# The scores of a whole batch: two pairs of heads per turn instead of one, in a cross-attention and FFN layer

## The chip, the core and the metric

The kernel runs on one core of one Trainium2 chip. The metric is the device time of one execution in microseconds (us). The engines are TensorE (PE in the profile, its weight loads PEld), VectorE (DVE), ScalarE (ACT), GpSimd (POOL) and SyncE (SP), which issues most of the DMAs.

## What is computed

A transformer layer on 32 batches of 100 rows of 256 values: cross attention of 16 heads of 64 over 361 context rows, then a feed-forward part of 1024 with int8-style quantization, each behind a layer norm and with a residual. Only the attention matters here:

```python
def _L0_xattn_ref(Q, K, V, WQ, WK, WV, WO, mask):
    B, T, D, H, DK, DV = (4, 512, 256, 16, 64, 64)
    Qh = jnp.einsum('btd,hdk->bhtk', Q, WQ)
    Kh = jnp.einsum('btd,hdk->bhtk', K, WK)
    Vh = jnp.einsum('btd,hdv->bhtv', V, WV)
    dk = jnp.asarray(Qh.shape[-1], Qh.dtype)
    logits = jnp.einsum('bhtk,bhsk->bhts', Qh, Kh) / jnp.sqrt(dk)
    logits = logits + mask * -1000000000.0
    attn = jax.nn.softmax(logits, axis=-1)
    Ah = jnp.einsum('bhts,bhsv->bhtv', attn, Vh)
    A = jnp.transpose(Ah, (0, 2, 1, 3)).reshape(Ah.shape[0], Ah.shape[2], -1)
    return A @ WO
...
x = x + _L0_xattn_ref(_layernorm(x, axis=-1), ctx_1024, ctx_1024, L0_xattn_WQ, ...
x = x + _L0_ffn_ref(_layernorm(x, axis=-1), L0_ffn_W1, L0_ffn_b1, L0_ffn_W2, L0_ffn_b2)
return x
```

x is (32, 100, 256), the context (32, 361, 256), the mask (1, 1, 100, 361); all of the attention is in float32.

## The kernel before

The heads are taken as eight pairs (NHP = 8), one head of a pair on SBUF partitions 0 to 63, the other on 64 to 127. The work on the batches is cut into 36 steps: batches 1 to 30 are one step each with all eight pairs ("whole-batch steps", n == NHP), batch 0 is three steps of 2, 2 and 4 pairs, batch 31 three of 4, 2 and 2. The loop over the steps (L616) issues for each step, in this order: scores(i), attend(i - 1), the values v of this batch (v_part), queries and projections where they are due, and the keys of the next step (k_part). TensorE runs its instructions in exactly this written order (manual_schedule at L598); the other engines' queues are ordered by the compiler, with extra edges from follow(a, b), which puts a behind b on its engine.

One softmax is spread over two steps. In step i, scores(i) multiplies queries and keys (tile sc, L423), adds the mask and takes the row's extreme on VectorE (tiles p and m, L434), takes exponentials on ScalarE (L404) and scales them by the reciprocals of their sums on VectorE (L443, L449). Before attend can multiply with v, the probabilities have to be transposed: weights_T(i - 1, pair) does this one step later, on TensorE (tile pt, L373), 12 transposes of a pair into two tiles, and copies the two tiles to SBUF (pT, L385), both copies on ScalarE, but the first of pair 0 on VectorE. p is one buffer for all pairs: the masked scores of a pair go where the transposes of the same pair of the step before have just read.

A whole-batch step works in turns (turns is true): in each turn the transposes of one pair of the step before, then the scores of one pair of this one, eight times. The step after one of four pairs (step 3, batch 1) has transposes in its first four turns only. In the smaller steps all transposes come first, and then the scores, two pairs (PAIRS = 2) at a time. In whole-batch steps the exponentials of all 16 heads come after the last turn, and each follows the last ScalarE copy of the transposes (copied, L408).

All PSUM tiles of the attention come from one pool of eight banks (L162, function bank at L191), one bank for each tile whatever its size. A tile beyond the eighth waits until an earlier one has been read for the last time: pt by its copy (L385), sc by the mask instruction (L434), which ends with a read of its accumulator into m.

A score product of one head is two instructions in the profile (two passes of a float32 product), so one pair's scores are x4; the two heads of a pair run side by side on the two halves of the array's rows, and so do two of a pair's transposes.

Of the kernel before, what the change touches and what calls it, by code (L numbers as in the profile page):

```python
# [27 lines left out]
def kernel(  # L28
# [31 lines left out]
    PAIRS = 2  # L60
# [34 lines left out]
    def follow(a, b):  # L95

        tc.add_manual_dep(a.ins, b.ins.name, ORDER)
# [61 lines left out]
    with ExitStack() as att:  # L159
# [31 lines left out]
        def bank(name):  # L191
            return psum.tile([P, 512], F32, tag="ps", name=name)
# [50 lines left out]
        for b in range(B):  # L243
            first = 0
# [118 lines left out]
        def weights_T(i, pair, on_vector):  # L363

            h0 = 2 * pair
            pts = [bank(f"pt{i}_{pair}_{k}") for k in range(2)]
            for h in range(2):
                for c in range(NSC):  # L370
                    for k in range(2):
                        ks = slice(k * RH, k * RH + TH)
                        nc.tensor.transpose(  # L373
                            pts[k][:SC, (h * NSC + c) * TH : (h * NSC + c + 1) * TH],
                            pb[ks, h0 + h, c * SC : (c + 1) * SC],
                            ident[ks, ks],
                        )
            pT = pTs[i, pair] = p1.tile(
                [SC, 2 * NSC, 2, TH], F32, tag=f"pT{pair}", name=f"pT{i}_{pair}"
            )  # L380
            copies = []
            for k in range(2):
                src = pts[k][:SC, : 2 * NSC * TH].rearrange("p (c t) -> p c t", t=TH)
                copy = nc.vector.tensor_copy if k == 0 and on_vector else nc.scalar.copy
                copies.append(copy(pT[:, :, k, :], src))  # L385
            return copies

        def scores(i):

            b, first, n = steps[i]
            g, j = b // G, b % G
            _, p0, before = steps[i - 1] if i else (0, 0, 0)
            turns = n == NHP
            heads = range(2 * first, 2 * (first + n))
            rsum = small.tile([TP, 2 * NHP], F32, tag="rsum", name=f"rsum{i}")
            r = small.tile([TP, 2 * NHP], F32, tag="r", name=f"r{i}")
            ms = {}

            def exponentials(heads):
                for h in heads:
                    s = pb[:, h, :S]
                    done = nc.scalar.activation(  # L404
                        s, s, AF.Exp, bias=ms[h], scale=-1.0, accum_out=rsum[:, h : h + 1]
                    )
                    if turns:
                        follow(done, copied)  # L408

            if not turns:  # L410
                for pair in range(p0, p0 + before):
                    weights_T(i - 1, pair, True)
            for pairs in ([q] for q in range(first, first + n)) if turns else (
                range(q, q + PAIRS) for q in range(first, first + n, PAIRS)
            ):
                if turns and pairs[0] < before:
                    copied = weights_T(i - 1, p0 + pairs[0], pairs[0] == 0)[1]
                pss = {}
                four = range(2 * pairs[0], 2 * pairs[-1] + 2)
                for h in four:  # L420
                    pair, k = divmod(h, 2)
                    pss[h] = bank(f"sc{i}_{h}")
                    nc.tensor.matmul(  # L423
                        pss[h][:TP, :S],
                        qbuf[pair // PAIRS][
                            k * DK : (k + 1) * DK, pair % PAIRS, j, :, :
                        ].rearrange("p k t -> p (k t)")[:, :TP],
                        kT[k * DK : (k + 1) * DK, pair, :],
                        start=True,
                        stop=True,  # L430
                    )
                for h in four:
                    ms[h] = small.tile([TP, 1], F32, tag=f"m{h}", name=f"m{i}_{h}", bufs=1)
                    found = nc.vector.tensor_tensor_reduce(  # L434
                        pb[:, h, :S], pss[h][:TP, :S], maskt, 1.0, BIG, ALU.add, ALU.min, ms[h]
                    )
                if not turns:
                    exponentials(four)
            if turns:
                exponentials(heads)  # L440
            at_once = 1 if i == len(steps) - 1 else 4
            for h0 in heads[::at_once]:
                last = nc.vector.reciprocal(  # L443
                    r[:, h0 : h0 + at_once], rsum[:, h0 : h0 + at_once]
                )
                follow(last, found)
                for h in range(h0, h0 + at_once):
                    s = pb[:, h, :S]
                    nc.vector.tensor_scalar(s, s, r[:, h : h + 1], None, ALU.mult)  # L449
            return last  # L450

        def attend(i, pairs=None):


            b, first, n = steps[i]
            if pairs is not None:
                first, n = pairs
            g, j = b // G, b % G
            if first == 0 and j == 0:
                aTs[g] = p1.tile([P, NHP, G, T], F32, tag="aT", name=f"aT{g}")  # L460
            for p0 in range(first, first + n, HP):
                m = min(HP, n)
                av = bank(f"av{i}_{p0}")
                for pair in range(p0, p0 + m):
                    for c in range(NSC):
                        for k in range(2):
                            h = 2 * (pair % HP) + k
                            nc.tensor.matmul(  # L468
                                av[k * DK : (k + 1) * DK, (pair - p0) * T : (pair - p0 + 1) * T],
                                vs[b, pair // HP][:, c, h * DK : (h + 1) * DK],  # L470
                                pTs[i, pair][:, k * NSC + c, :, :].rearrange("p k t -> p (k t)"),
                                start=(c == 0),
                                stop=(c == NSC - 1),
                            )
                copied = nc.scalar.copy(
                    aTs[g][:, p0 : p0 + m, j, :],
                    av[:, : m * T].rearrange("p (c t) -> p c t", t=T),
                )
            return copied
# [136 lines left out]
        for i, (b, first, n) in enumerate(steps):  # L616
            g, j = b // G, b % G
            begun = [h for h in range(2) if first <= h * HP < first + n]
            ended = [h for h in range(2) if first < (h + 1) * HP <= first + n]
            last = scores(i)  # L620
            if i >= 1:
                attend(i - 1)
            if b >= 1:
                for h in begun:
                    for c in range(NSC):
# [3 lines left out]
                        if c != 2:  # L629
                            copied = done  # L630
# [33 lines left out]
        i = len(steps) - 1  # L664
# [5 lines left out]
        copied = attend(i, (NHP - 1, 1))  # L670
# [167 lines left out]
    for u, (g, n) in enumerate(units):  # L838
# [3 lines left out]
        for fc in range(NFC):  # L842
# [36 lines left out]
            if (u, fc) in rounded:  # L879
                i = rounded[u, fc]  # L880
# [125 lines left out]
```

## Time and profile before

| | us |
|---|---|
| median of 3 runs | 1338.23 (1337.56 to 1338.39) |
| the profiled execution | 1336.85 |
| its span, first to last instruction | 1335.1 |
| mean granted TensorE clock | 0.995 of full speed |

The costliest groups on TensorE, with the number of instructions, busy time and mean of one:

| line, work | instructions | busy us | mean ns |
|---|---|---|---|
| L287 v, 128x512 | 768 | 338.3 | 596 |
| L256 k, 128x361 | 1016 | 314.2 | 467 |
| L423 sc, 64x361 | 1024 | 208.5 | 490 |
| L468 av, 128x100 | 3072 | 140.0 | 250 |
| L373 pt, 50x50 | 3072 | 133.5 | 221 |

Matmuls overlap one another in the records, so that busy times and means are longer than what an instruction adds to the time; the distance from one start to the next is what counts. A whole-batch step's scores, from the first transpose to the first matmul of attend, take 8.31 us in 29 of the 30 steps (625.27 to 633.58 for batch 16) and 6.66 us in step 3 (from 56.49). VectorE's masks in them are 512 instructions in all (16 a batch) with a mean of 533 ns and an accumulator read of 82 ns each; ScalarE's copies of pt are 462 with a mean of 413 ns, VectorE's 50 with 468 ns.

The page gives busy time of each engine and its share of the span; the chain of waits follows the work that ended last back to the start, and can be cut to a stretch of time; the time line lists instructions in order of start, merged where equal ones follow each other (xN), with an engine's idle time before them and what ended it in brackets.

### The profile page before, as it was taken

Reading aid. Unit: us, or ns where it says so; the run is one execution under the profiler, and the core shown is the slowest. Engines: PE = TensorE matmul, PEld = TensorE weight load, DVE = VectorE, ACT = ScalarE, POOL = GpSimd, SP = SyncE. Lnnn points to the kernel's source line nnn. Section 1 sums busy time; section 2 is a strip of 40 time slices with the busy share of each in tenths; the row PEclk is TensorE's granted clock in tenths of the full one; section 3 lists DMA queues with packets and bytes.
Section 4 is the critical chain, followed back from the end, with each engine's and each line's share of the span. In section 5 each row is a group of like instructions: output and inputs, shape, how many; then the busy total and the mean of one; then the engine's idle time right before and its main releaser. Section 6 shows DMA issues by size and latency. Waiting matters only on the chain.

```text
span 1335.1 us, 25493 instructions
## 1 busy us (share of the span) xinstructions
PE 1306.2 (98%) x10062; PEld 807.5 (60%) x10064; DVE 774.2 (58%) x2404; ACT 695.8 (52%) x1927; POOL 113.6 (9%) x198
## 2 busy tenths in 40 slices
PE   9999999999999999999999999999999999999858
PEld 4666556666566566666566666665666665666426
DVE  4666446664366554664366653664556643576897
ACT  2555345565355455562456453553455543554875
POOL 1000000200011000110011000110001100110260
PEclk9999999999999999999999999999999999999999
DMA  8010001000000000000000000000000000000112
GB/s 247 28 44 13 12 12 44 20 17 1 12 19 18 12 12 1 19 19 12 13 18 19 12 2 12 18 18 12 12 2 18 19 13 12 11 11 4 49 54 99
DMA packets 24864, 33.02 MB, mean 25 GB/s; under 512 B 1828, under 2 KB 22792, under 8 KB 24744
## 3 DMA queue, kind: packets, MB, share of 16 engines
q1 hardware_dynamic: 21776, 24.81, 6.3%
q0 software_dynamic: 2144, 5.38, 1.3%
q8 instruction: 79, 1.29, 0.4%
q10 hardware_dynamic: 824, 1.19, 0.3%
q14 instruction: 41, 0.34, 0.1%
HBM read 24.82 MB, written 6.55 MB: 24 GB/s over the span
## 4 chain that ended last, share of the span: by engine, by line
PE 94%; POOL 2%; issue 2%; ACT 1%; DVE 1%; POOLq 0%; DVEq 0%
PE pv L287 25%; PE pk L256 23%; PE sc L423 13%; PE av L468 10%; PE pt L373 7%; PE pq L348 6%; PE py L505 6%; PE pf L950 2%; PE po L489 1%; ACT h L860 1%; POOL r L797 1%; POOL r L798 1%; PE po L519 0%; PE ptx L336 0%; PE ph L852 0%
## 5 line engine op out<-in xcount | busy, mean ns | idle before, releaser
L287 PE MATMUL pv<-wvt,c 128*128 128x512 f32 x768 | 338.3, 596 | 0.0
L256 PE MATMUL pk<-c,wkt 128*128 128x361 f32 x1016 | 314.2, 467 | 0.0
L263 ACT COPY kT<-pk 128x361 f32<-128x361 f32 x254 | 116.8, 460 | 366.6 <-PE pk L256 366.6
L404 ACT ACTIVATE p<-p,m 114x361 f32<-114x361 f32 x512 | 297.4, 592 | 7.8 <-DVE m L434 7.8
L256 PEld LDWEIGHTS pk<-c,wkt 128*128 128x128 f32 x1016 | 191.9, 190 | 113.2 <-issue 1.0
L434 DVE CUSTOM_DVE_ANT_0 p<-sc,maskt 114x361 f32<-114x361 f32 x512 | 252.2, 533 | 11.9 <-PE sc L423 6.9
L287 PEld LDWEIGHTS pv<-wvt,c 128*128 128x128 f32 x768 | 143.3, 190 | 172.1 <-issue 161.9
L385 DVE COPY pT<-pt 128x300 f32<-128x300 f32 x50 | 22.3, 468 | 351.6 <-PE pt L373 351.6
L423 PE MATMUL sc<-kT,q 64*114 64x361 f32 x1024 | 208.5, 490 | 0.0
L385 ACT COPY pT<-pt 128x300 f32<-128x300 f32 x462 | 168.7, 413 | 74.1 <-PE pt L373 71.4
L373 PEld LDWEIGHTS pt<-ident,p 50*128 50x128 f32 x3072 | 131.1, 139 | 78.1 <-issue 51.5
L449 DVE TENSOR_SCALAR p<-p,r 114x361 f32<-114x361 f32 x512 | 173.5, 403 | 2.6
L294 DVE COPY v<-pv 128x512 f32<-128x512 f32 x192 | 129.4, 680 | 28.6 <-PE pv L287 28.3
L468 PEld LDWEIGHTS av<-pT,v 128*64 128x64 f32 x3072 | 132.8, 137 | 18.5 <-ACT pT L385 15.0
L468 PE MATMUL av<-pT,v 128*64 128x100 f32 x3072 | 140.0, 250 | 0.0
L373 PE MATMUL pt<-ident,p 50*128 50x50 f32 x3072 | 133.5, 221 | 0.3 <-DVE p L449 0.3
L135 POOL TENSOR_TENSOR xb<-x,b2a 100x256 f32<-100x256 f32 x32 | 23.4, 732 | 900.4 <-DVE rmax L529 891.2
L404 ACT ACTIVATION_READ_ACCUMULATOR p<-p,m 114x1 f32 x512 | 99.7, 195 | 0.0
L348 PE MATMUL pq<-xnT,wqt 128*128 128x400 f32 x256 | 87.9, 500 | 0.2 <-ACT xnT L339 0.2
L423 PEld LDWEIGHTS sc<-kT,q 64*114 64x114 f32 x1024 | 76.8, 184 | 4.3 <-issue 0.6
L505 PE MATMUL py<-aT,wot 128*128 128x400 f32 x224 | 76.4, 499 | 0.0
L443 DVE RECIPROCAL r<-rsum 114x4 f32<-114x4 f32 (+1 forms) x131 | 22.8, 175 | 90.2 <-ACT p L404 89.9
(131 smaller groups left out, 730.7 us busy)
## 6 DMA issues: line engine op xcount, KB each, us to landing
c<-in_ctxT_dram SPq DMA_DIRECT2D x31, 361.0 KB, 3.1
x<-in_x_dram SPq DMA_DIRECT2D x8, 400.0 KB
xb<-xb POOLq DMA_DIRECT2D x32, 100.0 KB, 2.1
x<-xb SPq DMA_DIRECT2D x5, 384.0 KB, 3.0
out_dram<-ot SPq DMA_DIRECT2D x3, 384.0 KB, 2.5
wqt<-in_wq_dram SPq DMA_DIRECT2D x4, 256.0 KB
wot<-in_wo_dram SPq DMA_DIRECT2D x1, 1024.0 KB, 8.9
w<-in_w1T_dram POOLq DMA_DIRECT2D x1, 1024.0 KB, 5.4
```

What stands on the lines that cost most here:

```text
L256: nc.tensor.matmul(pk[:, :S], wkt[q][:, dc, col * P : (col + 1) * P], c[:, dc, :S], start=(dc == 0), stop=(dc == NDC - 1),)
L287: nc.tensor.matmul(pv[:SC, :], c[:, dc, s * SC : (s + 1) * SC], wvt[h][:, dc, :], start=(dc == 0), stop=(dc == NDC - 1),)
L294: return nc.vector.tensor_copy(vs[b, h][:, s, :], pv[:SC, :])
L348: nc.tensor.matmul(pq[:, :GT], wqt[q][:, dc, pair * P : (pair + 1) * P], xnTs[g][:, dc, :], start=(dc == 0), stop=(dc == NDC - 1),)
L373: nc.tensor.transpose(pts[k][:SC, (h * NSC + c) * TH : (h * NSC + c + 1) * TH], pb[ks, h0 + h, c * SC : (c + 1) * SC], ident[ks, ks],)
L385: copies.append(copy(pT[:, :, k, :], src))
L404: done = nc.scalar.activation(s, s, AF.Exp, bias=ms[h], scale=-1.0, accum_out=rsum[:, h : h + 1])
L423: nc.tensor.matmul(pss[h][:TP, :S], qbuf[pair // PAIRS][k * DK : (k + 1) * DK, pair % PAIRS, j, :, :].rearrange("p k t -> p (k t)")[:, :TP ...
L434: found = nc.vector.tensor_tensor_reduce(pb[:, h, :S], pss[h][:TP, :S], maskt, 1.0, BIG, ALU.add, ALU.min, ms[h])
L449: nc.vector.tensor_scalar(s, s, r[:, h : h + 1], None, ALU.mult)
L468: nc.tensor.matmul(av[k * DK : (k + 1) * DK, (pair - p0) * T : (pair - p0 + 1) * T], vs[b, pair // HP][:, c, h * DK : (h + 1) * DK], pTs[i ...
L505: nc.tensor.matmul(py[:, :GT], wot[:, c, dc * P : (dc + 1) * P], aT[:, c, :, :].rearrange("p j t -> p (j t)"), start=(c == 0), stop=(c == ...
```

## The change

In whole-batch steps the loop over single pairs becomes a loop over groups of PAIRS = 2, as in the smaller steps. A turn then issues the transposes of two pairs of the step before (24), and then the scores of two pairs (8 score passes into four tiles), and there are four turns. Step 3 has transposes in its first two turns. copied is the last copy of the second pair of the turn. Nothing else is touched: the instructions are the same ones, in another order on TensorE.

```diff
@@ -410,11 +410,10 @@
             if not turns:
                 for pair in range(p0, p0 + before):
                     weights_T(i - 1, pair, True)
-            for pairs in ([q] for q in range(first, first + n)) if turns else (
-                range(q, q + PAIRS) for q in range(first, first + n, PAIRS)
-            ):
+            for pairs in (range(q, q + PAIRS) for q in range(first, first + n, PAIRS)):
                 if turns and pairs[0] < before:
-                    copied = weights_T(i - 1, p0 + pairs[0], pairs[0] == 0)[1]
+                    for pair in pairs:
+                        copied = weights_T(i - 1, p0 + pair, pair == 0)[1]
                 pss = {}
                 four = range(2 * pairs[0], 2 * pairs[-1] + 2)
                 for h in four:
```

## The prediction

> **What bounds the kernel now.** I read the page's busy table and its chain of waits first, then the chain cut to one batch, then the time lines of the engines in that batch's scores.
>
> ```profile
> PE 1306.2 (98%) x10062; PEld 807.5 (60%) x10064; DVE 774.2 (58%) x2404; ACT 695.8 (52%) x1927; POOL 113.6 (9%) x198
> PE 94%; POOL 2%; issue 2%; ACT 1%; DVE 1%; POOLq 0%; DVEq 0%
> ```
>
> TensorE is busy for 98% of the span and is 94% of the chain that ends last; no other engine passes 58%. A nanosecond counts if TensorE works less, or comes to wait. The chain through one whole-batch step (start, length, work):
>
> ```profile
> 626.51 0.36 PE pt L373 x12
> 626.87 0.66 PE sc L423 x4
> 627.53 0.36 PE pt L373 x12
> 627.89 0.66 PE sc L423 x4
> ```
>
> A turn is 12 transposes (0.36 us) and one pair's scores (0.66): 1.02 us, eight times, with no wait. The steps of the first and last batch already do what the change wants, so the same chain, cut there, prices it:
>
> ```profile
> 1217.70 1.63 PE pt L373 x48
> 1219.33 1.27 PE sc L423 x8
> ```
>
> Two pairs' scores in one run take 1.27, not 2 x 0.66 = 1.32. Now the engines that free the banks, VectorE (masks) and ScalarE (copies), on the time line:
>
> ```profile
> 626.54 0.54 DVE L434 CUSTOM_DVE_ANT_0 p<-sc,maskt 114x361 f32<-114x361 f32 x1 [0.19 <-PE sc L423]
> 627.00 0.08 DVE L434 DVE_READ_ACCUMULATOR2_ANT m<- 114x1 f32 x1
> 627.00 0.53 DVE L434 CUSTOM_DVE_ANT_0 p<-sc,maskt 114x361 f32<-114x361 f32 x1
> 627.46 0.08 DVE L434 DVE_READ_ACCUMULATOR2_ANT m<- 114x1 f32 x1
> 627.57 0.54 DVE L434 CUSTOM_DVE_ANT_0 p<-sc,maskt 114x361 f32<-114x361 f32 x1
> ```
> ```profile
> 626.96 0.72 ACT L385 COPY pT<-pt 128x300 f32<-128x300 f32 x2 [0.58 <-PE pt L373]
> ```
> ```profile
> 626.35 0.39 PEld L373 LDWEIGHTS pt<-ident,p 50*128 50x128 f32 x10 [0.16 <-issue]
> 626.64 0.30 PEld L423 LDWEIGHTS sc<-kT,q 64*114 64x114 f32 x4
> 627.07 0.14 PEld L373 LDWEIGHTS pt<-ident,p 50*128 50x128 f32 x2
> ```
>
> Masks of one pair start 0.46 apart; the next pair's starts 0.57 later, because it waits for its scores. Two heads cost VectorE 0.91 of a 1.02 turn: it keeps up, with a tenth to spare. A mask is over, and its bank free, 0.54 after its start (0.46 and the 0.08 read of the accumulator). The last line shows two transposes' weights loading while scores still stream, so 10 loads, not 12, are left for the transposes' own stretch.
>
> **What the Trainium skill says.** "PSUM — Partial Sum Buffer", Specifications (TRN2): 8 banks of 512 fp32 values per partition; its four rules let one matmul output fill one bank at most. The trace's tiles (300 and 361 columns) take a bank each, and the pool has eight. "TensorE: Matmul & The Clock Gate", Part 3 (What overlaps and what doesn't): weight loads overlap running matmuls where their row groups differ, matmuls stay in order. The trace agrees: loads at 627.07 under scores that run to 627.37; so a load held by a bank holds all that follows on TensorE. "TensorEngine Tiling (Array Packing)", PSUM Bottleneck: packing speeds TensorE, not the emptying of PSUM. The trace agrees: in a run, a pair's scores take (1.27 - 0.66) = 0.61, its masks 0.91.
>
> **The change part by part.** It touches the 30 steps with all eight pairs (batches 1 to 30). Instruction counts, DMAs and the DVE and ACT instructions stay; SP's and POOL's queues are not touched. Only TensorE's order changes: 24 transposes, then 8 score passes, per turn. Step 3, after a step of four pairs, transposes in two turns only.
>
> *Scores.* Joining two pairs saves 1.32 - 1.27 = 0.05.
>
> *Transposes.* In a long run 96 take 3.03 (1199.98 to 1203.01 on TensorE's time line), 0.38 per 12, against 0.36 now: two loads no longer hide under scores. Costs 0.02. Net gain per joint 0.03 to 0.04, I take 0.035. There are 4 in each of 29 steps and 2 in step 3: 118 x 0.035 = 4.1 us, if nothing waits.
>
> *Banks, the term that decides.* A turn now uses four banks (2 pt, 2 sc), so a bank has two turns to come free. Afterwards a turn uses four pt and four sc, all eight, and the fourth score bank of a turn must be empty before the fourth scores of the next. That wait is not in the trace of before; I build it from its rows. Zero is the step's first transpose:
> - Turn 0: transposes 0.79 (28.28 to 29.07 in an early step of two pairs), scores from 0.79. The first mask follows the scores' start by 0.86 (625.68 to 626.54): 1.65, then 2.10, 2.56, 3.01. Fourth bank free at 3.01 + 0.54 = 3.55.
> - Turn 1: transposes at 0.79 + 1.27 = 2.06, taking 0.74 (0.36 + 0.38); scores from 2.80; their second pair is due 0.66 later, at 3.46. But its bank is free at 3.55.
> - To that comes a restart d. A load that waited for VectorE started 0.06 after it ended (1249.25, after 1248.84 + 0.35). From a scores' load to the matmul is another 0.06 (625.62 to 625.68), and the first pass of a group shows 0.05 more than the others (0.66 - 0.61). d is 0.06 to 0.17. The wait is 0.09 + d: 0.15 to 0.26. I take 0.25, because nothing preloads a held load.
> - Turn 2: masks of turn 1 restart with its scores, at 2.80 + 0.86 = 3.66, so its fourth bank is free at 5.57; the second pair is due at 3.46 + 0.25 + 0.61 + 0.74 + 0.66 = 5.72, and with d the bank gives 5.57 + 0.15 = 5.72. No wait: the delay of turn 1 has paid for it.
> - Turn 3: the masks of turn 2 are again in step with its scores, so it waits like turn 1: 0.25.
>
> Per step: 2 x 0.25 - 4 x 0.035 = +0.36, times 29 = 10.4. Step 3: one wait, two joints: +0.18. Sum +10.6 us.
>
> *Costed at nothing.* The first pair of a turn needs banks free at 2.19 and 2.65 for scores at 2.80: cover 0.15 less restart; were it gone, d would be added to each turn. Copies: ScalarE makes four per turn in about 1.4 (0.36 each) of 2.0; the last bank is free near 2.0, the next turn's second pair needs it at 2.06 + 0.36. Exponentials stand behind the last copy (follow, L408), which ends some 0.2 earlier, and their 16 x 0.58 = 9.3 us still lie beside attend, v and k work of over 20 us. Masks end later, but the reciprocals behind them wait for exponentials anyway. In front of the held load nothing can pass; behind it stand the other scores, the next transposes, attend: the wait is paid in full.
>
> The profiled execution took 1336.85 (span 1335.1 and 1.75 around it): it becomes 1347.4. The median shown lies 1.38 above, so 1338.23 + 10.6 = 1348.8.
>
> **Rivals.** *Banks dealt in another order: faster.* Place: the fourth score tile of turns 1 and 3. Which bank it gets is settled when the program is built, by which bank is expected free first. If that is the first pt bank of the same turn, copied at about 2.06 + 1.03 = 3.09 (turn start 626.35, copies 626.96 on, about 0.42 each), it is free before 3.46: no wait, -4.1 us, 1334.1. It decides when the build expects that copy before the turn's last mask. For it: on the chip the copy (3.09) does come before the mask's end (3.55). Against it: the bank numbers in the program of before go round in strict order of use, last mask ahead of the next turn's first copy, although on the chip that copy ends first (627.98 + 0.41 = 628.39 against a mask ending 628.56). So the build expects VectorE earlier, or TensorE later, than the chip has them.
>
> *VectorE sets the pace of every turn: slower still.* If turn 2 waits as well, because its margin above is 0.00, and the wait is 0.27: 3 x 0.27 - 0.14 = 0.67 x 29, about +19.5: 1357.7. For it: no margin. Against it: the arithmetic of turn 2 holds for every d.
>
> That the change doesn't do what it says I exclude: the two loops differ in the grouping alone.
>
> **How the numbers follow.** Two waits per step: 0.70, at 1348.8; its own range is 1343 (d of 0.06: 2 x 0.15 - 0.14 = 0.16 x 29 = 4.7) to 1352. Other banks: 0.20, at 1334.1. Three waits: 0.10, at 1357.7. The range of 8 in 10 takes the first and third case, 1342 to 1358, and leaves the other banks out. About 0.2% (2.7 us) is what a measurement here can tell from no change. Slower: 0.80 less 0.03 for waits so short that the sum falls below that: 0.77. Same 0.03. Faster 0.20.
>
> **What would show it.** Right: in whole-batch steps the score passes of the second pair in turns 1 and 3 start late by 0.15 to 0.27, with the loads' releaser DVE L434; the step from first transpose to first attend matmul grows from 8.31 to 8.6-8.8; runs of 24 transposes take 0.74 and unheld runs of 8 scores 1.27. Wrong: the step is 8.1 to 8.2 with no TensorE idle at L423 (other banks), or L423 waits in three turns, or a wait at the transposes for ScalarE's copies.

## The result and the profile after

The changed kernel takes 1342.01 us (median of 7 runs, 1341.64 to 1343.29), the kernel before 1337.56 beside it (7 runs): a ratio of 1.0035, with a 95% interval of 1.0025 to 1.0045. It is slower, by 4.5 us, and the forecast was 1348.8. The profiled execution took 1342.01, its span is 1340.2. The page's busy table and the shares of the chain of waits, where lines after the edited loop now have numbers one lower (scores L422, masks L433, attend L467):

```profile
PE 1311.9 (98%) x10064; PEld 836.6 (62%) x10064; DVE 768.8 (57%) x2404; ACT 685.2 (51%) x1927; POOL 113.9 (9%) x198
PE 94%; ACT 2%; issue 2%; POOL 2%; DVE 0%; POOLq 0%; DVEq 0%
```

TensorE is busy for 98% again. The loss stands in no row of idle time, only in TensorE's own length (1306.2 before). Its place is found with the distance from a step's first transpose to attend's first matmul: 8.45 us instead of 8.31 in 29 whole-batch steps, 6.83 instead of 6.66 in step 3. Over the 30 steps that is 251.99 against 247.61, and these 4.4 us are the measured difference but for 0.1. The chain cut to one such step (batch 16; start, length, work):

```profile
627.79 0.88 PE pt L373 x24
628.67 1.27 PE sc L422 x8
629.94 0.73 PE pt L373 x23
630.67 1.31 PE sc L422 x8
631.99 0.75 PE pt L373 x20
632.73 0.06 PE sc L422
632.79 0.12 PE pt L373 x2
632.92 1.12 PE sc L422 x7
```

Turns are counted from 0. Where before stretches of 0.36 and 0.66 alternated, 24 transposes take 0.73 and 8 score passes 1.27: the joints came as priced. From 631.99 on, transposes and scores are mixed, in an order that nobody wrote. TensorE's time line shows why:

```profile
628.51 1.43 PE L422 MATMUL sc<-kT,q 64*114 64x361 f32 x8
...
630.51 1.68 PE L422 MATMUL sc<-kT,q 64*114 64x361 f32 x8
631.78 0.95 PE L373 MATMUL pt<-ident,p 50*128 50x50 f32 x21
632.57 0.52 PE L422 MATMUL sc<-kT,q 64*114 64x361 f32 x1
632.57 0.35 PE L373 MATMUL pt<-ident,p 50*128 50x50 f32 x3
632.76 1.43 PE L422 MATMUL sc<-kT,q 64*114 64x361 f32 x7
```

The first line is turn 0's scores, the second turn 1's: the same eight, but 1.68 instead of 1.43, so one of them came 0.25 late. Yet turn 2's transposes start at 631.78, where they would start without a wait (4.06 after the step's first), and the first score pass of turn 2 starts before the last three transposes of its turn. The array's rows have two halves, one for each head of a pair (lower is the first head's), and here they run apart: the lower half is on time, the upper one, whose load was held, is behind by four transposes. The trace doesn't name the half of an instruction; here and below it is told from the order of issue and from the distances between starts. What held it, on the time lines of VectorE and of TensorE's weight loads:

```profile
630.74 0.53 DVE L433 CUSTOM_DVE_ANT_0 p<-sc,maskt 114x361 f32<-114x361 f32 x1
631.19 0.08 DVE L433 DVE_READ_ACCUMULATOR2_ANT m<- 114x1 f32 x1
...
633.42 0.54 DVE L433 CUSTOM_DVE_ANT_0 p<-sc,maskt 114x361 f32<-114x361 f32 x1 [0.15 <-PE sc L422]
```
```profile
631.32 0.17 PEld L422 LDWEIGHTS sc<-kT,q 64*114 64x114 f32 x1
```
```profile
631.48 0.13 PEld L373 LDWEIGHTS pt<-ident,p 50*128 50x128 f32 x1
```

The first mask here is the last of turn 0; its accumulator read ends at 631.27, and 0.05 later starts the load of turn 1's last score tile, which gets that bank. The last line of VectorE's is the first mask of turn 2. It starts 5.70 after the step's first transpose. The last load shown is the first one that the lower half needs for turn 2, 0.16 after the held one. In all that follows, times within a step are counted from its first transpose. The starts of the two passes of each half's second pair of scores, with what they would be without a wait (lower half's, or that plus 2.00 a turn):

| | lower half | upper half | without a wait |
|---|---|---|---|
| turn 1 | 3.45, 3.76 | 3.61, 4.00 | 3.45, 3.76 |
| turn 2, first pair's first pass | 4.85 | 5.04 | 4.79 |
| turn 3, second pair | 7.51, 7.82 | 7.70, 8.06 | 7.45, 7.76 |

The upper half loses 0.24 in turn 1, nothing in turn 2 (its four passes take 0.97 as in turn 0), and 0.05 in turn 3, where the last pass is 8.06 instead of 7.70 + 0.31 (its first load starts 0.05 after an accumulator read again: 7.61 and 7.66). The joints give 0.15, as the second run below shows. 0.24 + 0.05 - 0.15 = 0.14, and the step grew by 8.452 - 8.308 = 0.144.

Why the busy table is blind to this is seen in the instructions of the tile (durations in ns, least, median and greatest, of the same step):

```profile
L422 PE MATMUL sc<-kT,q x32: 461/464/556, 628.5 to 635.8; 64*114 64x361 f32 x32
```

A pass is on record for 464 ns, though the next one of its half starts 0.31 us later. The upper half's pass before the held one starts at 3.15, so its record ends at 3.61, where the held pass starts: the hold leaves no gap. The held pass has 556 ns, since its record starts with its own load and so counts the loading as work. And the other half works on.

### The profile page after: what moved, and what is told of

Same layout as the page of the kernel before. It is cut to its first block, busy times and chain, and to the rows that moved or that the text cites. A ratio compares the mean times of both kernels' runs of the same rounds, so it can differ in the third digit from the quotient of the medians.

```text
span 1340.2 us, 25500 instructions
## 1 busy us (share of the span) xinstructions
PE 1311.9 (98%) x10064; PEld 836.6 (62%) x10064; DVE 768.8 (57%) x2404; ACT 685.2 (51%) x1927; POOL 113.9 (9%) x198
## 4 chain that ended last, share of the span: by engine, by line
PE 94%; ACT 2%; issue 2%; POOL 2%; DVE 0%; POOLq 0%; DVEq 0%
PE pv L287 25%; PE pk L256 23%; PE sc L422 12%; PE av L467 10%; PE pt L373 8%; PE pq L348 6%; PE py L504 6%; PE pf L949 2%; ACT h L859 2%; PE po L488 1%; POOL r L796 1%; POOL r L797 1%; PE po L518 0%; ACT xqT L779 0%; PE ptx L336 0%
## 5 line engine op out<-in xcount | busy, mean ns | idle before, releaser
L433 DVE CUSTOM_DVE_ANT_0 p<-sc,maskt 114x361 f32<-114x361 f32 x512 | 242.5, 531 | 28.5 <-PE sc L422 22.2
L422 PE MATMUL sc<-kT,q 64*114 64x361 f32 x1024 | 202.4, 481 | 0.0
L385 ACT COPY pT<-pt 128x300 f32<-128x300 f32 x462 | 158.1, 421 | 75.1 <-PE pt L373 72.5
L467 PEld LDWEIGHTS av<-pT,v 128*64 128x64 f32 x3072 | 132.8, 137 | 18.6 <-ACT pT L385 15.0
L467 PE MATMUL av<-pT,v 128*64 128x100 f32 x3072 | 140.0, 250 | 0.0
L373 PE MATMUL pt<-ident,p 50*128 50x50 f32 x3072 | 128.4, 223 | 0.3 <-DVE p L448 0.3
L422 PEld LDWEIGHTS sc<-kT,q 64*114 64x114 f32 x1024 | 110.6, 180 | 26.5 <-issue 0.6
L404 ACT ACTIVATION_READ_ACCUMULATOR p<-p,m 114x1 f32 x512 | 103.6, 202 | 0.0
L348 PEld LDWEIGHTS pq<-xnT,wqt 128*128 128x128 f32 x256 | 48.4, 190 | 38.8 <-issue 3.9
```

Of the source, the lines that this page charges most:

```text
L348: nc.tensor.matmul(pq[:, :GT], wqt[q][:, dc, pair * P : (pair + 1) * P], xnTs[g][:, dc, :], start=(dc == 0), stop=(dc == NDC - 1),)
L373: nc.tensor.transpose(pts[k][:SC, (h * NSC + c) * TH : (h * NSC + c + 1) * TH], pb[ks, h0 + h, c * SC : (c + 1) * SC], ident[ks, ks],)
L404: done = nc.scalar.activation(s, s, AF.Exp, bias=ms[h], scale=-1.0, accum_out=rsum[:, h : h + 1])
L422: nc.tensor.matmul(pss[h][:TP, :S], qbuf[pair // PAIRS][k * DK : (k + 1) * DK, pair % PAIRS, j, :, :].rearrange("p k t -> p (k t)")[:, :TP ...
L433: found = nc.vector.tensor_tensor_reduce(pb[:, h, :S], pss[h][:TP, :S], maskt, 1.0, BIG, ALU.add, ALU.min, ms[h])
L467: nc.tensor.matmul(av[k * DK : (k + 1) * DK, (pair - p0) * T : (pair - p0 + 1) * T], vs[b, pair // HP][:, c, h * DK : (h + 1) * DK], pTs[i ...
```

## Experiments

In this section "the step" is a whole-batch step of the 29. The kernel before was timed again beside each group of runs, on the same chip.

**Is the bank wait the whole loss?** The eight banks are given out by hand in the first two runs: the control goes round in strict order of use, which is what the program of the changed kernel has; the other gives the fourth score tile of a turn the bank of the turn's first transpose tile, which is copied earlier than the last mask is done.

Control:

```diff
-        def bank(name):
+        order = list(range(8))
+        def bank(name, n=None):
+            n = order[0] if n is None else n
+            order.remove(n)
+            order.append(n)
-            return psum.tile([P, 512], F32, tag="ps", name=name)
+            return psum.tile([P, 512], F32, tag=f"ps{n}", name=name, bufs=1)
```

> The changed kernel with its eight banks dealt by hand in strict order of use, as a control for the dealing by hand. All theories: as the changed kernel, a step of 8.45 us, some 4.4 us more than before, with the fourth score load of turn 1 held by VectorE for about 0.15 us.

Measured: 1342.31 us against 1337.36, ratio 1.0036 (1.0022 to 1.0049); step 8.46, with the same starts as above. It stands for the changed kernel.

Other bank, control plus:

```diff
+                    early = order[1] if turns and pairs[0] < before and h == four[-1] else None
-                    pss[h] = bank(f"sc{i}_{h}")
+                    pss[h] = bank(f"sc{i}_{h}", early)
```

> Banks are dealt by hand: the fourth score tile of a turn takes the bank of that turn's first transposes instead of the bank of the last mask of the turn before. Theory 'one half waits' (the only loss of the change is the fourth score load held by the last mask, and it holds the upper half of the array alone): no held load, a whole-batch step of 8.16 us (8.45 with the change, 8.31 before), so 29 x -0.15 - 0.1, some 4.4 us less than before. Theory 'all of TensorE waits' expects the same here. Rival 'the grouping itself costs' (longer runs of transposes and scores lose the time, whatever bank they write): still 8.45, 4.4 us more than before.

Measured: 1332.77 us, ratio 0.9965 (0.9951 to 0.9979), step 8.157, step 3 6.58. The chain in one step has no late part:

```profile
623.22 0.88 PE pt L378 x24
624.10 1.27 PE sc L428 x8
625.37 0.73 PE pt L378 x24
626.10 1.27 PE sc L428 x8
627.38 0.73 PE pt L378 x24
628.11 1.27 PE sc L428 x8
```

This version is faster than both kernels. All that the regrouping costs is the wait for one bank; without it the joints give 8.308 - 8.157 = 0.15 a step, 4.4 us in all.

The same by the other route, with the banks of the changed kernel and the masks shortened to 280 of 361 columns, and the exponentials behind them too, first in the changed kernel and then in the kernel before (one execution each):

```diff
+            M = 280 if turns else S
...
-                    s = pb[:, h, :S]
+                    s = pb[:, h, :M]
...
-                        pb[:, h, :S], pss[h][:TP, :S], maskt, 1.0, BIG, ALU.add, ALU.min, ms[h]
+                        pb[:, h, :M], pss[h][:TP, :M], maskt[:, :M], 1.0, BIG, ALU.add, ALU.min, ms[h]
```

> The changed kernel with masks and exponentials of whole-batch steps cut to the first 280 of 361 columns; the other columns keep older numbers, so the softmax is another one. A mask then takes VectorE about 0.37 instead of 0.455 us, and the last one of a turn is over 0.34 earlier. Theories of a bank wait: no held load, a step of 8.16, some 4.4 us less than before. Rival 'the grouping itself costs': 8.45, 4.4 us more than before.

> The kernel before with masks and exponentials of whole-batch steps cut to 280 of 361 columns, the same part left out as in the run with short masks above. Every theory has VectorE off the chain here: a step of 8.31 and the time of before within 1.5 us. If short masks are a gain in themselves (some 4 us or more less than before), the run with short masks says nothing of banks.

Measured: the changed kernel 1332.17 us with a step of 8.157, the kernel before 1336.80 with 8.308. Both kernels leave out the masks and exponentials of the last 81 columns. Shorter masks and exponentials are worth nothing by themselves, and they remove the loss. The exponentials come only after the last turn, so it is the masks: the wait is for VectorE.

**Why is the second wait not paid?** The forecast had two full waits in a step. The theory from the trace: a held load makes its own half of the rows late and not the other, as long as the other needs no load before the hold is over. If the held load is the third of a turn's four, the fourth, which is the other half's and due at the same time, stands behind it, and both halves are late. The control with the banks of a turn's last two score tiles exchanged for the next turn:

```diff
+                if turns:
+                    order[-2:] = order[:-3:-1]
```

> As the control, but the third score tile of a turn (lower half of the array) takes the bank of the last mask, and the fourth the bank of the third. The same bank comes free at the same moment, but the held load now stands ahead of both halves. Theory 'one half waits': both halves are held, the masks of turn 2 restart late, and turn 3 waits again: 8.16 + 0.24 + 0.03 + 0.24, a step of 8.65 to 8.7, some 10 us more than before. Rival 'all of TensorE waits' at either load: no difference from the control, 8.45 and 4.4 us more than before. Rival 'the grouping itself costs': 8.45 too.

Measured: 1347.01 us, ratio 1.0071 (1.0057 to 1.0084), step 8.65. The chain in one step:

```profile
631.18 0.88 PE pt L378 x24
632.06 1.27 PE sc L427 x8
633.33 0.73 PE pt L378 x24
634.06 1.52 PE sc L427 x8
635.58 0.73 PE pt L378 x24
636.31 1.27 PE sc L427 x8
637.59 0.73 PE pt L378 x24
638.32 1.51 PE sc L427 x8
```

1.27, 1.52, 1.27, 1.51: both halves together, two full waits of 0.25 in turns 1 and 3 and none in turn 2. This is the forecast's own arithmetic (8.31 + 0.36 = 8.67) in the kernel for which it holds. Here TensorE's weight loads do stand idle, and the profile names what they waited for, the accumulator read of the last mask (turn 1's last four loads):

```profile
634.72 0.28 PEld L427 LDWEIGHTS sc<-kT,q 64*114 64x114 f32 x4 [0.58 <-DVE m L440]
```

So a held load does hold a load of the other half that is issued behind it. In the changed kernel it reaches nothing of the lower half: that half's next load starts at 3.76 (631.48), as in the run without a wait (626.91, also 3.76), and the held one has started by then, at 3.60. Whether a hold that lasts longer would stop the lower half too, no run shows.

Two further runs were to separate "third or fourth" from "lower or upper", by issuing the upper head of a turn's last pair first, with the control's banks and with the last two exchanged:

```diff
-                for h in four:
+                for h in (*four[:-2], four[-1], four[-2]) if turns else four:
                     pair, k = divmod(h, 2)
```

> As the control, but the scores of a turn's last head (upper half of the array) are issued third and those of the head before it (lower half) fourth; masks keep their order. The load that waits for the last mask is now the third issued, for the upper half. If what counts is its place in TensorE's order (a held load holds what is issued behind it, and as the third it holds both halves): a step of 8.65, some 10 us more than before, as with the lower half held third. If what counts is which half of the array is held: 8.45, 4.4 us more than before.

> The same order of issue, with the banks of the last two score tiles exchanged, so that the held load is the fourth issued, for the lower half. By place in the order: 8.45, 4.4 us more than before. By half of the array: 8.65, 10 us more.

Measured: 1347.34 us, ratio 1.0075 (1.006 to 1.009), step 8.64; and 1347.28, ratio 1.0074 (1.0057 to 1.0091), step 8.66. Their traces say that they are not the kernels that they were meant to be: another load was held in each than was meant. That fits if VectorE's masks followed the new order of issue, so that the bank that comes free last went to another tile; the trace doesn't tell the masks of a turn apart. In the first it was the fourth load that was held, of the lower half (passes at 3.61 and, for the upper half, on time at 3.45); in the second the third, of the upper half, with the fourth behind it (both at 3.61), which is the swap again. So the second run confirms the swap, and the first is new: one half held, as in the control, and still 8.64. Its halves start turn 2's scores at 4.92 (upper) and 5.04 (lower), and the first mask of turn 2:

```profile
636.22 0.54 DVE L438 CUSTOM_DVE_ANT_0 p<-sc,maskt 114x361 f32<-114x361 f32 x1 [0.34 <-PE sc L427]
```

With the step's start at 630.32 that is 5.90, not 5.70: 0.86 after the late lower half's scores. Not that one half runs free decides, then, but whether the masks of turn 2 may start with it. A mask start of 5.90 gives a bank at 5.90 + 3 x 0.455 + 0.55 = 7.82 and a second full wait (that pass starts at 7.86), one of 5.70 a bank at 7.62, before the pass is due at 7.70.

**Which half has to be on time?** First the control with only the order of the masks changed, so that the half that is late is masked first; follow holds VectorE to that order:

```diff
+                masked = None
-                for h in four:
+                for h in (four[1], four[0], *four[2:]) if turns else four:
...
+                    if turns and masked is not None:
+                        follow(found, masked)
+                    masked = found
```

> As the control on TensorE, but in each turn of a whole-batch step VectorE masks the upper head of the first pair before the lower one. The held load of turn 1 is still the fourth, and the upper half is still the late one. Theory 'the late half must not be the one masked first' (a second wait comes only where the first mask of turn 2 has to wait for the late half): the masks of turn 2 start 0.2 later, turn 3 waits again, a step of 8.65, some 10 us more than before. Rival 'only the place of the held load in TensorE's order counts': as the control, 8.45 and 4.4 us more than before.

Measured: 1347.83 us, ratio 1.0078 (1.0063 to 1.0093), step 8.69; the same single held load, of the upper half, and the masks of turn 2 start at 5.94. The second wait is back (last pair of turn 3 at 7.90).

Then the other way round, the lower half late (issued last) and the upper half masked first: the issue order of the run above, and masks in the order four[1], four[0], four[3], four[2].

> The scores of a turn's last pair in reversed order (upper head third, lower fourth) and the masks in the order upper, lower, upper, lower. The held load is the fourth, for the lower half; the half that is masked first is on time. Theory 'the late half must not be the one masked first': no second wait, 8.45 to 8.5, some 4.4 to 6 us more than before. Rival 'a late lower half is what costs': 8.65, as in the run before with the lower half late and masked first.

Measured: 1348.58 us, ratio 1.0082 (1.0066 to 1.0099), step 8.70. A miss. The upper half's scores of turn 2 start at 4.96, but their mask only at 5.95, which is 5.08 + 0.87: it waited for the lower head's scores too. In the trace the score products raise one counter, on which the masks wait. A mask that is to go first but whose product was issued second waits for both.

So the issue order of the first pair was changed as well, to upper, lower, upper, lower, and in a second kernel the transposes too, upper half first:

```diff
-                for h in (*four[:-2], four[-1], four[-2]) if turns else four:
+                for h in (four[1], four[0], four[3], four[2]) if turns else four:
```
```diff
-                    for k in range(2):
+                    for k in (1, 0) if 2 <= i < 32 else (0, 1):
                         ks = slice(k * RH, k * RH + TH)
```

> Scores of a turn issued upper, lower, upper, lower and masked in the same order; transposes as before (lower half's first). The held load is the fourth issued, now of the lower half. Theory 'VectorE sees the score products in order of issue, so the second wait stays small whenever the half that is issued and masked first is the one that is not held': masks of turn 2 start about 5.70 from the step's first transpose, the hold in turn 3 is under 0.1, step 8.45 to 8.50, some 1342.3 to 1343.5. Rival 'a late lower half is what costs (its transposes stand first in the queue, so both halves follow it)': the second wait returns, step 8.65 to 8.70, some 1347 to 1348.5.

> As the run before it, and the transposes too are issued upper half's first: lower and upper half have changed places in everything but the copies. Theory of order of issue: 8.45 to 8.50 as well, at most 0.05 below the run before it. Rival 'only the halves' places in the array count': 8.65 or more. If the run before is at 8.65 and this one at 8.45, it is the transposes' order that decides.

Measured: 1344.15 us, ratio 1.0047 (1.0032 to 1.0062), step 8.52; and 1342.38, ratio 1.0035 (1.0022 to 1.0048), step 8.45. The first mask of turn 2 in the first of them, whose step starts at 629.26:

```profile
635.04 0.54 DVE L439 CUSTOM_DVE_ANT_0 p<-sc,maskt 114x361 f32<-114x361 f32 x1 [0.22 <-PE sc L427]
```

5.78 instead of 5.95, by the issue order of one pair. It missed its expectation: the step by 0.02 and the time by 0.65 at the upper end, the masks of turn 2 start at 5.78 and not at about 5.70, and the hold in turn 3 is 0.12 and not under 0.1. With the transposes turned round too, the mirror image has the control's times within 0.01. Neither half is special. The runs in one table, by the start of turn 2's masks (us from the step's first transpose):

| run | late half | turn 2: scores of the head that the first mask waits for | first mask of turn 2 | held pass in turn 3 | step |
|---|---|---|---|---|---|
| control | upper | 4.85 | 5.70 | 7.70 | 8.45 |
| mirror | lower | 4.84 | 5.70 | 7.70 | 8.45 |
| upper issued first | lower | 4.92 | 5.78 | 7.74 | 8.52 |
| upper issued third | lower | 5.04 | 5.90 | 7.86 | 8.64 |
| banks exchanged | both | 5.04 | 5.90 | 7.86 | 8.65 |
| late half masked first | upper | 5.08 | 5.94 | 7.90 | 8.69 |
| late half issued first, masked second | lower | 5.08 | 5.95 | 7.92 | 8.70 |

The step follows the start of these masks. In the last two rows the first wait is 0.04 longer as well: in every turn their first mask waits for the second product (1.69 instead of 1.65 in turn 0).

## Why the prediction was right or wrong

*That it is slower, and where: right.* The fourth score tile of turn 1 waits for the last mask of turn 0, since a turn now goes round all eight banks, and with this wait gone the loss is gone. The releaser that was to show it stands in no row of the changed kernel, because the loads of the other half run on; it does in the run with banks exchanged.

*Joints: right.* 0.05 and 0.02 gave 0.14 a step; without the wait 0.15 was measured, 4.4 us where 4.1 was forecast.

*The banks' order, turn 1 and turn 2: right.* The build gave the banks out in strict order of use. The bank came free at 3.55 as forecast, the hold was 0.24 (0.25 forecast), and turn 2 waited for nothing.

*Step 3: right.* One wait and two joints were to cost 0.18; the step grew by 6.825 - 6.661 = 0.16.

*Turn 3: wrong, and this is the step that failed.* "The masks of turn 2 are again in step with its scores, so it waits like turn 1: 0.25." It paid 0.05. The sentence rests on another one, that behind the held load "the other scores, the next transposes, attend" stand and "the wait is paid in full". That put the delay of one load on both halves of the rows. The held load was the last of its turn, and over before the other half needed its next one; from there that half's transposes and scores went on ahead of the late half's, VectorE masks its head first, and the masks of turn 2 began at 5.70 rather than at the 5.92 which the forecast's delay of all scores gives. So turn 3's bank came free at 7.61 and not at 7.83. The step grew to 8.45, where 8.6 to 8.8 was named as the sign of being right. In the run with banks exchanged, where the held load is followed by the other half's in the same turn, that step of the forecast holds and the kernel takes 1347.01.

The sum with this one term put right: 29 x (0.24 + 0.05 - 0.15) = 4.1, and 0.16 for step 3, 4.2 on the 1337.56 of the kernel before: 1341.8, against 1342.01. Of the forecast's surplus of 6.8, 29 x (0.25 - 0.05) = 5.8 is this term; what is left is the base, since the first three runs of the kernel before had a median 0.67 higher, and some hundredths a step in the other terms. That 1342.01 still lies at the low edge of the forecast's 1342 to 1358 is luck: that edge stood for two waits of 0.15, and not for one full wait and a small one.

On this point the Trainium skill was read too broadly, and its sentence doesn't fit either. "TensorE: Matmul & The Clock Gate", Part 3 (What overlaps and what doesn't) has matmuls in strict order of start and end. In this trace a score pass started at 632.57, before three transposes that were issued ahead of it, so the order does not hold across the halves; that it holds within a half would fit the starts, but the trace doesn't name the halves. The measurement decides. Nor did the loads at 627.07 bear the forecast out: transposes alternate between the halves, so the two loads are one of each half, while the scores of both halves run until 627.37. They say nothing of row groups that differ, and nothing of what a held load holds.

*The rivals.* Banks dealt otherwise: it isn't what the build did, but made by hand it gives what was worked out for it: 4.6 us less than the 1337.36 beside it, where 4.1 less was forecast. Three waits: no run shows one in turn 2.

Left open: the wait was removed by giving one tile another bank and by shorter masks. A ninth bank there is not, and whether fewer or shared transpose banks would do as well wasn't tried. Why the lower half, which was not held, starts turn 2's scores 0.06 late (4.85 for 4.79), no run shows.

## What to carry to other kernels

Joining two stages saves their seam (here 0.15 in a step of four joints), but it also shortens the distance, counted in buffers, between a buffer's last reader and its next writer: before grouping, count the tiles of a turn against the pool, and give the last tile of a turn the buffer whose reader finishes first, not the one used longest ago. When work runs side by side on parts of TensorE, ask of a wait which part it makes late and whether the next engine in the ring can go on with the other part; here a held load that was the last of its turn, and of the part consumed second, cost 0.24 once and 0.05 later, and one ahead of both parts 0.25 each time. And a wait of this kind is found by start-to-start distances, since the busy table stays at 98%.

## What was not expected of the hardware

- The two halves of the array's rows keep separate time: after one held load they ran 0.24 us (four transposes) apart over a whole turn of 24 transposes, with starts out of the written order across the halves, and the lag shrank to 0.19 by the next scores.
- A score load that waited for VectorE started 0.05 after the accumulator read had ended (631.27 to 631.32). Its half's two passes then start 0.39 apart instead of 0.31, so that a hold of 0.16 at the first pass is one of 0.24 at the second.
